# Relational graph layer on one core: A11 B11 by quarters in matrices one to three, index keys fetched earlier, and a new order for the fifth pair of row blocks

## The chip, the cores and the metric

The kernel runs on one core of one Trainium2 chip. The metric is the device time of one execution in microseconds (us), lower is better. TensorE is called PE below, VectorE DVE, ScalarE ACT, GpSimd POOL and SyncE SP, as in the profile.

## The reference

There are N = 1250 nodes with D = 1024 features, 20000 edges (src, dst) sorted by dst, and R = 8 edge types. Cut to what matters:

```python
h = maximum(layernorm(x), 0)
u = h @ root + bias
for r in range(8):                       # per type: mean over incoming edges, then a matrix
    mean_r = segment_sum(h[src] * (type == r), dst) / maximum(count_r, 1)
    u = u + mean_r @ weight[r]
z = concatenate([u, h]) @ w_gate + b_gate
out = x + tanh(u) * z + h * (1 - z)
```

All data are float32.

## The kernel before

**Matrices and steps.** The mean over edges is exchanged with the product: the kernel multiplies h with every weight matrix first, writes the results to DRAM (`y`), and then gathers the rows that the edges name. There are eleven 1024x1024 matrices, `mats`, numbered s: the eight weights (0 to 7), `root` (8), the lower half of `w_gate` (9) and its upper half (10, multiplied with u in a last stage of its own). h has ten blocks of 128 rows. They are taken as NP = 5 pairs, i = 0 to 4; pair i holds blocks i and i + 5. `step(s, i)` multiplies pair i with matrix s, and the order is s outside, i inside. The text writes step (s, i).

**One step.** `product` multiplies 256x1024 by 1024x1024 by the scheme of Strassen and Winograd: seven products of half size instead of eight. They are A11 B11, S1 T1, S2 T2, S4 B22, S3 T3, A12 B21 and A22 T4. The S are sums of quarters of h, made once (`h_op`); the T are differences of quarters of the matrix, made by DVE for each matrix (`make_t1` to `make_t4`). `p1` to `p7` in the code are these products in Winograd's numbering: p1 = A11 B11, p5 = S1 T1, p6 = S2 T2, p3 = S4 B22, p7 = S3 T3, p2 = A12 B21, and A22 T4 comes last. Each is `add`, line L404: four matmuls with 512 moving columns, which the profile shows as eight instructions (f32 goes through in two). The results go to the four quarters c11, c12, c21, c22 of two `row` tiles `t[0]`, `t[1]`: copies out of PSUM by ACT (c11 L452, c22 L463, c12 L483, the piece d of c22 L428, c21 L513), additions by DVE (L421, L429, L443).

**Second level.** For matrices s > 0, pairs 0 and 1 are joined, and pairs 2 and 3 (`paired`), so that one of the seven products of both can be split once more into seven products of quarter size (256 moving columns, line L217) instead of eight. `Second` does so for A12 B21 in matrices 1 to 9. `Third` does it for S4 B22 and `First` for A11 B11, before the change only in matrices s > EARLY = 3. Pair 4 has no partner. `First` is worked in two halves: `early()` (four quarter products) at the end of the step before, `late()` (three) in place of A11 B11 of the even step; the odd step finds its A11 B11 ready in PSUM. Its sums of matrix and of h (`sums`, `next_sums`, four DVE operations each) go to the tiles `room`.

**PSUM.** There are four banks `ps`, two `ps_b` (the running sum b that begins with A11 B11), one `ps_n`, one `ps_q`. In matrices 0 to 3, `ps_q` belongs to the index work below.

**Calls.** All engines' instructions are in program order (the schedule is by hand). After each product `done()` calls `between(j)`, j = 0 to 6 in each step. There the other work is put in: loads of the next matrix (`load_first`, `load_next`, `load_b22`, `load_b21`), its differences, the sums, and one piece of a generator.

**Index work.** In matrices 0 to 3 that generator is `index()`: it turns the edge list into a table of slots. `slots` handles the 157 columns of edges in 40 groups of four, one group in two calls. The first call of two has `one_hots` (ACT, L1023 and L1025) and `load_keys` (SP: `k_bc` and `l_bc`, 256 KB each); the second has on PE `look` (L1091) and `count` (L1037), and on DVE `pick` (L1099), `add_counts`, `residue` (L1076) and `place` (L1107, L1112); `to_los` (ACT, L1083 and L1084) turns `l_bc` into the one-hots `to_lo` that `look` of the same group multiplies in the next round. Then `order` ranks the nodes by their number of edges (`places`, twenty DVE operations L1175) and `rows_and_weights` has POOL scatter the ids and gather the table rows. From matrix 5 on the generator is `edges`: POOL gathers rows of `y` (L1315), and DVE adds them with weights (L1320).

**Places of a matrix.** `load_first` gives each matrix nine buffers in rotation; in the version before, B21 takes the buffer of the old B22, and T4 that of the old T3.

Of the kernel before, what the change touches and what calls it, by code (L numbers as in the profile page):

```python
# [19 lines left out]
def tile_rgcn_highway(  # L20
# [109 lines left out]
    class Factors:  # L130
# [55 lines left out]
    class Second:  # L186
# [22 lines left out]
        def left(self):  # L209
            nc.vector.tensor_add(self.s1, self.a21, self.a22)  # L210
# [177 lines left out]
    def product(aop, w, to, between=lambda j: None, last=None, pieces=1, whole=True,  # L388
                fill=None, second=None, third=None, inner=None, first=None, early=None, own=(),
                aside=None):  # L390
# [49 lines left out]
        def p2():  # L440
            a = held("ps_q")
            add(a, A12, True)
            nc.vector.tensor_add(c11, c11, a)  # L443
            done()

        def p1():
            if first is None:
                b = lead()
                add(b, A11, True)
            else:  # L450
                b = first.late() if inner.holds else first.to1
            nc.scalar.copy(c11, b)  # L452
            done()
            filled("first")
            return b

        def p5(c=None):
            if c is None:
                c = inner.hold() if inner and inner.holds else held("ps_n")
                add(c, S1, True)  # L460
            else:
                add(c, S1, ks=range(KQ // 2, KQ))
            nc.scalar.copy(c22, c)  # L463
            done()
            filled("fifth")
            return c

        if first and inner.holds and early is None and "first" not in fill:
            c = inner.hold()
            add(c, S1, True, ks=range(KQ // 2))  # L470
            b = p1()
            p5(c)
        elif first and inner.holds:
# [12 lines left out]
        if whole and not third:  # L486
            p3()
            d = p7()
            if not second:
                p2()  # L490
        else:
            def then():
                inner.then(c)
                done()
                filled("third")

            if early:
                then()
            d = p7()
            if third:  # L500
                last(d, 0)
            if not inner:
                p3()
            elif not early and not inner.holds:
                then()
        if early:
            early()
        if pieces == 1:
# [11 lines left out]
        done()  # L520
        filled("fourth")
# [27 lines left out]
    def step(s, i, between=lambda j: None, second=None):  # L549
# [23 lines left out]
        def beside(j):  # L573
            at_call[:] = i, j
            new = fac[s + 1]
            if i == 0 and s > 0 and j == int(thirds(s)):
# [11 lines left out]
            if coming and i > 1 and j == 2:  # L588
                first_sums()
            if two and (i, j) == (1, 6):  # L590
                Second(fac[s], 2).left()
            if (s, i, j) == (0, 0, 3) or (s > 0 and (i, j) == (3, int(thirds(s)))):
# [18 lines left out]
        def sums(j):  # L611
# [20 lines left out]
        if two:  # L632
# [46 lines left out]
            else:  # L679
# [4 lines left out]
                inner=q, first=waiting_first.get((s, i - i % 2)) if two else None,  # L684
                early=early if coming else None, own=("ps_q",) if s > EARLY and not two else ())
# [73 lines left out]
    def rows_and_weights(g):  # L759
# [16 lines left out]
        for d in range(ND):  # L776
            rows_of(idx[:, g, d, :], table_rows, node_key[:, g, d:d + 1])
            if d % 2:
                yield

    with ExitStack() as early:
# [155 lines left out]
        pid = ix1.tile([P, 1], F32, name="pid")  # L937
        less_pid = ix1.tile([P, 1], F32, name="less_pid")
# [6 lines left out]
        def columns():  # L945
# [54 lines left out]
            nc.vector.tensor_single_scalar(less_pid, pid, -1.0, op=OP.mult)  # L1000
            yield

        def slots(ix):
# [14 lines left out]
            def one_hots(j):  # L1018
# [13 lines left out]
                now[j] = dict(is_lo=is_lo, is_at=is_at)  # L1032
# [18 lines left out]
            def load_keys(j):  # L1051
                c0, m = j * CG, len(chunks(j))
                for name, of in (("k_bc", keys_dram), ("l_bc", los_dram)):
                    t = now[j][name] = ix.tile([P, CG, P], I32, name=name, bufs=3)
# [93 lines left out]
        def order():  # L1148

            with tc.tile_pool(name="sort", bufs=1) as sp:  # L1150

                nc.gpsimd.iota(ids, pattern=[[P, ND]], base=0, channel_multiplier=1)
                ids_f = sp.tile([P, ND], F32, name="ids_f")
                nc.vector.tensor_copy(ids_f, ids)
# [12 lines left out]
                for _ in range(4):  # L1167
# [3 lines left out]
                def places(g):  # L1171
                    for d in range(ND):
# [5 lines left out]
                        if d % 2:  # L1178
                            yield
                    nc.vector.tensor_copy(pos_i[:, g, :], pos[:, g * ND:(g + 1) * ND])  # L1180

                for g in range(G):
                    yield from places(g)
                    if g == 0:
                        for _ in rows_and_weights(0):
                            pass
# [92 lines left out]
    with ExitStack() as edges_part:  # L1279
# [4 lines left out]
        inner_pool = edges_part.enter_context(tc.tile_pool(name="inner", bufs=1))  # L1284
        room = [inner_pool.tile([P, 2, n], F32, name=f"inner{k}")
                for k, n in enumerate((H, H, P, P))]
        p5_room = inner_pool.tile([P, H], F32, name="inner4")
# [150 lines left out]
        def beside_group():  # L1438

            for _ in range(4):  # L1440
                yield
            passes_over()
            yield
            yield from rows_and_weights(1)
            yield
            yield
# [341 lines left out]
```

## Time and profile before

| | |
|---|---|
| time, median of 3 runs | 1342.91 us (1342.43 to 1347.58) |
| profiled execution: time, span | 1342.95 us, 1341.2 us (1.75 us lie outside the span) |
| granted PE clock in it | 0.998 |
| PE busy | 1328.3 us (99%), 4096 instructions |
| DVE busy | 931.1 us (69%) |
| ACT busy | 372.0 us (28%) |
| POOL busy | 573.8 us (43%) |
| DMA | 270.92 MB, 202 GB/s |

The profile is that of one execution. Its times are in microseconds from the start of the span. Ends of matmuls are modelled, since they overlap; so where PE's time is counted, the text takes the distance from one group's start to the next group's start. Step (1, 0) starts at about 139, matrix 4 at about 510, and the last stage at about 1208.

### The profile page before, as it was taken

What the parts mean: (1) busy time and instruction counts of PE and PEld (TensorE: products, weight loads), DVE (VectorE), ACT (ScalarE), POOL (GpSimd) and SP (SyncE); (2) the same over time, 40 slices, a digit from 0 to 9 for tenths busy, and PEclk for the clock granted to TensorE, in tenths of its full rate; (3) what the DMA queues carried; (4) which work ended last, traced back from release to release, by engine and by line L of the source; (5) the groups of instructions that cost most, each with busy time, mean ns of one, the idle gap of its engine ahead of it and who ended that gap; (6) DMA issues with size and microseconds to landing.
All of it is one profiled execution on the core that took longest, in us unless ns stands there. A gap on an engine that the chain in (4) does not pass through costs nothing.

```text
span 1341.2 us, 13172 instructions
## 1 busy us (share of the span) xinstructions
PE 1328.3 (99%) x4096; PEld 709.1 (53%) x4096; DVE 931.1 (69%) x1763; ACT 372.0 (28%) x786; POOL 573.8 (43%) x509
## 2 busy tenths in 40 slices
PE   9999999999999999999999999999999999999997
PEld 5444455455445545655655565565556556554443
DVE  7753744654572855347887978887778799867875
ACT  3334556465641111211121211122121111221210
POOL 0000454555556256201454645436355565725631
PEclk9999999999999999999999999999999999999999
DMA  8744487956872361133739778868778967879961
GB/s 313 275 182 158 85 138 154 215 87 110 168 177 30 101 172 46 51 127 126 246 118 334 236 251 324 313 222 279 274 265 297 344 202 241 287 272 286 345 170 59
DMA packets 104317, 270.92 MB, mean 202 GB/s; under 512 B 20100, under 2 KB 22354, under 8 KB 104112
## 3 DMA queue, kind: packets, MB, share of 16 engines
q1 hardware_dynamic: 44048, 119.85, 30.9%
q0 software_dynamic: 44064, 118.20, 28.1%
q10 hardware_dynamic: 16128, 31.98, 7.4%
q8 instruction: 32, 0.52, 0.2%
q14 instruction: 45, 0.37, 0.1%
HBM read 212.63 MB, written 75.49 MB: 215 GB/s over the span
## 4 chain that ended last, share of the span: by engine, by line
PE 89%; DMA 4%; issue 3%; DVE 2%; POOL 1%; ACT 0%; POOLq 0%; SPq 0%; DVEq 0%; ACTq 0%
PE ps_b L404 45%; PE ps L404 18%; PE ps L217 12%; PE ps_n L404 5%; PE ps_b L217 2%; PE ps_q L217 2%; PE ps_q L404 2%; PE ps_n L217 1%; DMA got<-y,idx 1%; DMA l_bc<-los_dram 1%; PE ps L369 1%; DMA hr_dram<-row 1%; DMA h_op<-in_L_gnn_b_gate_dram 0%; POOL out_dram L720 0%; DVE u L1320 0%
## 5 line engine op out<-in xcount | busy, mean ns | idle before, releaser
L404 PE MATMUL ps_b<-w,h_op 128*128 128x512 f32 x1560 | 701.9, 595 | 1.1 <-ACT row L483 0.8
L404 PEld LDWEIGHTS ps_b<-w,h_op 128*128 128x128 f32 x1560 | 291.6, 190 | 329.3 <-issue 318.0
L1315 POOL DMA_INDIRECT got<-y,idx x193 | 249.9, 1295 | 309.3 <-DVE u L1320 187.6
L1320 DVE SCALAR_TENSOR_TENSOR u<-got,w_of,u 128x1024 f32<-128x1024 f32 (+1 forms) x193 | 246.7, 1281 | 35.8 <-DMA got<-y,idx 33.3
L404 PE MATMUL ps<-w,h_op 128*128 128x512 f32 (+1 forms) x592 | 263.4, 588 | 1.0 <-ACT row L463 1.0
L1130 POOL DMA_INDIRECT table<-row_col,at_i x157 | 165.3, 1053 | 180.8 <-DVE at_i L1126 119.5
L404 PEld LDWEIGHTS ps<-w,h_op 128*128 128x128 f32 x592 | 111.3, 190 | 125.0 <-issue 120.8
L429 DVE TENSOR_TENSOR row<-row 128x512 f32<-128x512 f32 x53 | 36.6, 691 | 81.3 <-ACT row L428 81.2
L428 ACT COPY row<-ps_b 128x512 f32<-128x512 f32 x53 | 31.0, 585 | 199.5 <-PE ps_b L404 199.5
L513 ACT COPY row<-ps_b 128x512 f32<-128x512 f32 x49 | 28.6, 584 | 200.9 <-PE ps_b L404 179.7
L404 PE MATMUL ps_n<-w,h_op 128*128 128x512 f32 x176 | 80.1, 592 | 0.0
L217 PE MATMUL ps<-w,w 128*128 128x256 f32 x288 | 71.5, 381 | 0.2 <-DVE w L210 0.2
L483 ACT COPY row<-ps_b 128x512 f32<-128x512 f32 x54 | 31.6, 585 | 136.8 <-PE ps_b L404 136.6
L217 PE MATMUL ps<-w,h_op 128*128 128x256 f32 x264 | 68.3, 381 | 0.0
L217 PEld LDWEIGHTS ps<-w,w 128*128 128x128 f32 x288 | 54.2, 190 | 21.7 <-issue 14.3
L217 PEld LDWEIGHTS ps<-w,h_op 128*128 128x128 f32 x264 | 49.6, 190 | 24.3 <-issue 18.7
L1112 DVE SCALAR_TENSOR_TENSOR junk<-k_bc,key_col,before 128x128 f32<-128x128 int32 x157 | 54.9, 350 | 4.2
L452 ACT COPY row<-ps_b 128x512 f32<-128x512 f32 x54 | 31.7, 587 | 92.8 <-PE ps_b L404 87.1
L1099 DVE TENSOR_TENSOR own<-ps_q,is_at 128x160 f32<-128x160 f32 (+1 forms) x40 | 12.7, 317 | 62.4 <-PE ps_q L1037 58.1
L404 PEld LDWEIGHTS ps_n<-w,h_op 128*128 128x128 f32 x176 | 33.4, 190 | 39.5 <-issue 38.7
L463 ACT COPY row<-ps 128x512 f32<-128x512 f32 x37 | 21.6, 585 | 106.9 <-PE ps L404 96.8
L1023 ACT ACTIVATE is_lo<-io,less_lo 128x128 bf16<-128x128 f32 x157 | 50.1, 392 | 3.0 <-PE ps L404 2.3
(237 smaller groups left out, 1441.3 us busy)
## 6 DMA issues: line engine op xcount, KB each, us to landing
y<-row SPq DMA_DIRECT2D x72, 512.0 KB
w<-in_L_gnn_weight_dram ACTq DMA_DIRECT2D x21, 1024.0 KB
w<-in_L_gnn_weight_dram SPq DMA_DIRECT2D x10, 1024.0 KB
k_bc<-keys_dram SPq DMA_DIRECT2D x39, 256.0 KB
l_bc<-los_dram SPq DMA_DIRECT2D x39, 256.0 KB
w<-in_L_gnn_w_gate_dram ACTq DMA_DIRECT2D x6, 1024.0 KB
h_dram<-h_op SPq DMA_DIRECT2D x9, 512.0 KB
u<-in_L_gnn_bias_dram SPq DMA_DIRECT2D x9, 512.0 KB
```

What stands on the lines that cost most here:

```text
L217: nc.tensor.matmul(p, a[:, k, :], b[:, k, :], start=(fresh and k == 0), stop=(k == 1), skip_group_check=True)
L404: nc.tensor.matmul(b[:, at], aop[:, i, k, :], w.of[i][:, k, at], start=(fresh and k == 0), stop=(k == KQ - 1), skip_group_check=True)
L428: nc.scalar.copy(d, b)
L429: nc.vector.tensor_add(c22, c22, d)
L452: nc.scalar.copy(c11, b)
L483: nc.scalar.copy(c12, b)
L513: nc.scalar.copy(c21, b)
L1023: nc.scalar.activation(is_lo[:, i, :], io, AF.Abs, bias=less_lo[:, c0 + i:c0 + i + 1])
L1112: nc.vector.scalar_tensor_tensor(junk, o["k_bc"][:, i, :], key_col[:, c:c + 1], before, op0=OP.is_equal, op1=OP.mult, accum_out=rank[:, c: ...
L1130: ins = nc.gpsimd.indirect_dma_start(out=table[:, :], out_offset=bass.IndirectOffsetOnAxis(ap=at_i[:n, c:c + 1], axis=0), in_=row_col[:n, ...
L1315: nc.gpsimd.indirect_dma_start(out=t[:n], out_offset=None, in_=y[g][:, :], in_offset=bass.IndirectOffsetOnAxis(ap=at[:n, d, k:k + 1], axis=0),
L1320: nc.vector.scalar_tensor_tensor(u[:n], t[:n], w, u[:n], op0=OP.mult, op1=OP.add)
```

## The change

The change does the following.

1. `First` is used for all matrices s > 0 (`firsts`), so also for the pairs (0, 1) and (2, 3) of matrices 1, 2 and 3. `room` and `p5_room` move to a pool that lives all through. A new argument `head` (even step) takes the place of `inner.holds`.
2. The fifth pair, i = 4, has an order of its own in matrices 0 to 9 (`lone`): p1, p5, p6, the first half of A12 B21, S3 T3, the second half of A12 B21, `early` of the next matrix, A22 T4, and S4 B22 at the end. c22 is no longer copied out by ACT: DVE adds d to the bank c itself. B21 and T4 of a matrix change buffers.
3. The index work has its keys loaded two rounds earlier (`k_bc` in five buffers) and `to_los` one round earlier (`to_lo` in four). The ids are made in `columns`. `order` waits seven calls and not four, and ranks one column in a call and not two. `rows_and_weights(1)` follows at once and no longer stands in `beside_group`. Calls (1, 5) and (4, 4) get no index work; before, (4, 5) got none.
4. `Second.left` is cut in two. Its first two sums are made at call 3 (before: call 4 in matrices 1 to 3, call 5 after them), the other two at call 4 or 5. For s > 3, `right(2)` and `right(3)` move from call 4 to call 5. `make_t4` is at call 1 in all matrices s > 0 (before: call 0 in matrices 1 to 3).

The diff, cut to its core:

```diff
-                                  t2=p["t2"], b21=p["b22"], t4=p["t3"])
+                                  t2=p["t2"], b21=p["t3"], t4=p["b22"])
...
+        def next_left(self):
             nc.vector.tensor_sub(self.s3, self.a11, self.a21)
             nc.vector.tensor_sub(self.s4, self.a12, self.s2)
...
-            nc.vector.tensor_add(c22, c22, d)
+            nc.vector.tensor_add(c22, c if lone else c22, d)
...
-            nc.scalar.copy(c22, c)
+            if not lone:
+                nc.scalar.copy(c22, c)
...
-        if first and inner.holds and early is None and "first" not in fill:
-            c = inner.hold()
+        if first and head and early is None and "first" not in fill:
+            c = inner.hold() if inner else bank()
             add(c, S1, True, ks=range(KQ // 2))
             b = p1()
             p5(c)
...
-        if whole and not third:
+        if lone:
+            a = held("ps_q")
+            add(a, A12, True, ks=range(KQ // 2))
+            p7()
+            p2(a)
+        elif whole and not third:
...
         if early:
             early()
-        if pieces == 1:
+        if lone:
+            add(b, A22)
+            nc.scalar.copy(c21, b)
+            done()
+            p3()
+        elif pieces == 1:
...
+    def firsts(s):
+        return s > 0
...
-        if thirds(s) and i == 1:
+        if firsts(s) and i == 1:
             return s, 2
-        if thirds(s + 1) and i == NP - 1 and s + 1 < NM - 1:
+        if firsts(s + 1) and i == NP - 1 and s + 1 < NM - 1:
...
-            if i == 0 and s > 0 and j == int(thirds(s)):
+            if i == 0 and s > 0 and j == 1:
                 fac[s].make_t4()
...
-            if q and i % 2 == 0 and j == 3:
+            if two and i % 2 == 0 and j == 3:
                 waiting_first[s, i].fifth_to()
-                q.sums()
+                if i == 0:
+                    waiting[0][0].left()
+                if q:
+                    q.sums()
...
-            if coming and i > 1 and j == 2:
+            if coming and (i > 1 or not q) and j == 2:
                 first_sums()
...
-            for k in {2: (0, 1), 4: (2, 3)}.get(j, ()) if s > EARLY else (j,) if j < 4 else ():
+            for k in {2: (0, 1), 5: (2, 3)}.get(j, ()) if s > EARLY else (j,) if j < 4 else ():
                 e.right(k)
             if j == (5 if s > EARLY else 4):
-                e.left()
+                e.next_left()
...
-                for name, of in (("k_bc", keys_dram), ("l_bc", los_dram)):
+                for name, of, bufs in (("k_bc", keys_dram, 5), ("l_bc", los_dram, 3)):
...
-                to_lo = o["to_lo"] = ix.tile([P, CG, P], BF16, name="to_lo")
+                to_lo = o["to_lo"] = ix.tile([P, CG, P], BF16, name="to_lo", bufs=4)
...
+            load_keys(0)
             for j in range(ng + 3):
-                for f, of in ((one_hots, j), (load_keys, j - 1), (as_bf16, j - 2),
+                for f, of in ((one_hots, j), (load_keys, j + 1), (as_bf16, j - 2),
                               (None, None), (look, j - 3), (count, j - 1), (pick, j - 3),
                               (add_counts, j - 1), (residue, j - 2), (place, j - 3),
-                              (to_los, j - 2), (None, None)):
+                              (to_los, j - 1), (None, None)):
...
-                if s > 0 and (i, j) in ((0, 0), (NP - 1, 5)):
+                if s > 0 and (i, j) in ((0, 0), (1, 5), (NP - 1, 4)):
```

More of the change, by code (lines that the diff above doesn't have):

```diff
@@ L389, in product @@
                 fill=None, second=None, third=None, inner=None, first=None, early=None, own=(),
-                aside=None):
+                aside=None, head=False, lone=False):
         c11, c12 = to[0][:, :Q], to[0][:, Q:]
@@ L438, in held, with p2 @@
             return psum.tile([P, CG, P], F32, name=name, bufs=1).rearrange("p c k -> p (c k)")
-        def p2():
-            a = held("ps_q")
-            add(a, A12, True)
+        def p2(a=None):
+            if a is None:
+                a = held("ps_q")
+                add(a, A12, True)
+            else:
+                add(a, A12, ks=range(KQ // 2, KQ))
             nc.vector.tensor_add(c11, c11, a)
@@ L450, in p1 @@
             else:
-                b = first.late() if inner.holds else first.to1
+                b = first.late() if head else first.to1
             nc.scalar.copy(c11, b)
@@ L472, in product @@
             p5(c)
-        elif first and inner.holds:
+        elif first and head:
             c = p5()
@@ L485, in product @@
         filled("sixth")
-        if whole and not third:
+        if lone:
+            a = held("ps_q")
+            add(a, A12, True, ks=range(KQ // 2))
+            p7()
+            p2(a)
+        elif whole and not third:
             p3()
@@ L495, in then @@
                 filled("third")
-            if early:
+            if early and inner:
                 then()
@@ L503, in product @@
                 p3()
-            elif not early and not inner.holds:
+            elif not early and not head:
                 then()
@@ L519, in product @@
                 last(b[:, at], at.start, d[:, at])
-        done()
-        filled("fourth")
+        if not lone:
+            done()
+            filled("fourth")
     mats = [weight[r] for r in range(R)] + [root, w_gate[D:, :], w_gate[:D, :]]
@@ L591, in beside @@
                 Second(fac[s], 2).left()
+                Second(fac[s], 2).next_left()
             if (s, i, j) == (0, 0, 3) or (s > 0 and (i, j) == (3, int(thirds(s)))):
@@ L684, in step @@
                 inner=q, first=waiting_first.get((s, i - i % 2)) if two else None,
+                head=i % 2 == 0, lone=i == NP - 1,
                 early=early if coming else None, own=("ps_q",) if s > EARLY and not two else ())
@@ L779, in rows_and_weights @@
                 yield
+    room = [keep.tile([P, 2, n], F32, name=f"inner{k}") for k, n in enumerate((H, H, P, P))]
+    p5_room = keep.tile([P, H], F32, name="inner4")
     with ExitStack() as early:
@@ L937, in tile_rgcn_highway @@
         pid = ix1.tile([P, 1], F32, name="pid")
+        ids_f = ix1.tile([P, ND], F32, name="ids_f")
         less_pid = ix1.tile([P, 1], F32, name="less_pid")
@@ L1000, in columns @@
             nc.vector.tensor_single_scalar(less_pid, pid, -1.0, op=OP.mult)
+            nc.gpsimd.iota(ids, pattern=[[P, ND]], base=0, channel_multiplier=1)
+            nc.vector.tensor_copy(ids_f, ids)
             yield
@@ L1031, in one_hots @@
                                         op=OP.is_equal)
-                now[j] = dict(is_lo=is_lo, is_at=is_at)
+                now[j].update(is_lo=is_lo, is_at=is_at)
             def count(j):
@@ L1052, in load_keys @@
                 c0, m = j * CG, len(chunks(j))
-                for name, of in (("k_bc", keys_dram), ("l_bc", los_dram)):
-                    t = now[j][name] = ix.tile([P, CG, P], I32, name=name, bufs=3)
+                for name, of, bufs in (("k_bc", keys_dram, 5), ("l_bc", los_dram, 3)):
+                    t = now.setdefault(j, {})[name] = ix.tile([P, CG, P], I32, name=name,
+                                                              bufs=bufs)
                     nc.sync.dma_start(t[:, :m, :].rearrange("p c e -> p (c e)"),
@@ L1150, in order @@
             with tc.tile_pool(name="sort", bufs=1) as sp:
-                nc.gpsimd.iota(ids, pattern=[[P, ND]], base=0, channel_multiplier=1)
-                ids_f = sp.tile([P, ND], F32, name="ids_f")
-                nc.vector.tensor_copy(ids_f, ids)
                 val = sp.tile([P, NHI], F32, name="val")
@@ L1166, in order @@
                 nc.vector.memset(one, 1.0)
-                for _ in range(4):
+                for _ in range(7):
                     yield
@@ L1177, in places @@
                             op0=OP.is_gt, op1=OP.mult, accum_out=pos[:, c:c + 1])
-                        if d % 2:
-                            yield
+                        yield
                     nc.vector.tensor_copy(pos_i[:, g, :], pos[:, g * ND:(g + 1) * ND])
@@ L1183, in order @@
                     yield from places(g)
-                    if g == 0:
-                        for _ in rows_and_weights(0):
-                            pass
+                    for _ in rows_and_weights(g):
+                        pass
                 nc.vector.reduce_max(most[:, 0:1], runs, axis=AX.X)
@@ L1283, in tile_rgcn_highway @@
         drc = small.tile([P, ND], F32, name="drc")
[L1284 to L1287, printed above, removed]
         fresh = [GOT]
@@ L1438, in beside_group @@
         def beside_group():
-            for _ in range(4):
+            yield
+            passes_over()
+            for _ in range(5):
                 yield
[L1442 to L1446, printed above, removed]
             for g in range(G):
```

## The prediction

> **What bounds the kernel now.** I read the page's busy shares, then the groups, the waits of PE alone, the timeline by groups, and the chain where PE stood.
>
> ```profile
> PE 1328.3 (99%) x4096; PEld 709.1 (53%) x4096; DVE 931.1 (69%) x1763; ACT 372.0 (28%) x786; POOL 573.8 (43%) x509
> PE ps L404 <- ACT row L463: 1.0, 1, 1.0
> PE ps_q L1091 <- ACT to_lo L1084: 0.6, 1, 0.6
> PE ps L217 <- DVE w L210: 0.2, 1, 0.2
> ```
>
> The first line is the page: PE is busy for 99% of the span, no other engine for more than 69%. The other three are the waits of PE (line, releaser, us in total, times, longest): in all the matrices PE waits hardly at all, and three of its seven waits are at places that the change touches. So the time is the sum of PE's groups, plus these waits, plus what the change adds of new ones. The price of a group is its distance to the next one in the timeline (step (4, 4) and the start of (5, 0)):
>
> ```profile
> 615.68 3.60 PE L404 MATMUL ps_q<-w,h_op 128*128 128x512 f32 x8
> ...
> 619.11 1.03 PE L217 MATMUL ps<-w,h_op 128*128 128x256 f32 x4
> 619.97 1.03 PE L217 MATMUL ps<-inner,inner 128*128 128x256 f32 x4
> 620.84 1.03 PE L217 MATMUL ps_b<-w,h_op 128*128 128x256 f32 x4
> 621.70 1.03 PE L217 MATMUL ps<-inner,inner 128*128 128x256 f32 x4
> 622.56 3.60 PE L404 MATMUL ps_b<-w,h_op 128*128 128x512 f32 x8
> ...
> 627.71 1.03 PE L217 MATMUL ps<-inner,inner 128*128 128x256 f32 x4
> 628.58 1.03 PE L217 MATMUL ps_b<-w,inner 128*128 128x256 f32 x4
> 629.46 1.13 PE L217 MATMUL ps_b<-inner,h_op 128*128 128x256 f32 x4
> 630.42 1.88 PE L404 MATMUL ps_n<-w,h_op 128*128 128x512 f32 x4
> ```
>
> A product of eight instructions with 512 columns takes 619.11 - 615.68 = 3.43 us. The four groups from 619.11 are `early`, 3.45 us; the three from 627.71 are `late`, 2.71 us, of which 0.11 us is the wait of the third group for ACT's copy L353. That is `First` as matrices 4 to 9 run it already.
>
> **First in matrices 1 to 3.** Per joined pair two products A11 B11 go (2 x 3.43 = 6.87 us) and 3.45 + 2.71 = 6.16 us come: -0.71 us. Six pairs (two in each of three matrices): -4.2 us. A rule that speaks against it stands in the Trainium skill, "TensorE: Matmul & The Clock Gate", section "Back-to-back issue gap": spacing is set by the weight load as well as by the columns, about 81 ns at 128 and 131 ns at 512 columns. An estimate by a straight line between them puts 256 columns at 0.75 of the price of 512; then the seven small products would cost 28 x 0.75 x 0.429 = 9.0 us, every pair would lose 2.1 us, and the six 13 us. The row above has 0.216 us for 256 columns against 0.429 us for 512, a half; I go by the row.
>
> Beside PE the new work is per pair: DVE eight sums (2.2 us each four, rows L271 to L274), L348 and L360 of 0.43 us, together some 5.3 us; ACT two copies of 0.36 us and one of 0.57 us. Does it stay beside PE? In matrix 1 DVE was busy 17.3 of 22.8 us in step (1, 0), 10.1 of 23.0 us in the next and 13.1 of 30.0 us in the third stretch (busy time by stretches 139.2:162, 162:185, 185:215). The even step loses 0.72 us of PE and gains 0.4 us of DVE: 17.8 of 22. The odd step gets the sums of the next pair, 5.3 us: about 15 of 23. The deadlines: `next_sums` (2.2 us, after an addition of 0.43 us) must be done between the end of `early` and `late`. Between them lie A22 T4 and half of S1 T1, 3.43 + 1.72 = 5.15 us, after step 4 also S4 B22, 8.6 us. In calls (1, 5) and (4, 4) no index work is queued ahead of it. `make_t2` (2.28 us) is ahead of it in step 4; it hides under `early`. If that cover went, a late sum would cost up to 2.6 us each, 16 us for six.
>
> ACT is tighter. In step (s, 3) A11 B11 no longer stands first, and its copy c11 has to be out before S2 T2 may add to the bank. The timeline around 192 shows what is queued ahead of it:
>
> ```profile
> 192.21 0.58 ACT L452 COPY row<-ps_b 128x512 f32<-128x512 f32 x1 [1.87 <-PE ps_b L404]
> 192.69 1.28 ACT L1023 ACTIVATE is_lo<-io,less_lo 128x128 bf16<-128x128 f32 x4
> 194.00 0.63 ACT L1025 ACTIVATE is_lo<-is_lo 128x512 bf16<-128x512 bf16 x1
> 194.54 0.24 ACT L1069 CAST s_b<-seen 128x80 bf16<-128x80 f32 x1
> ```
>
> A copy starts 0.20 us after its product, one round of one-hots then ends 2.6 us later, `to_los` takes 0.72 + 0.63 us, c11 0.59 us: 4.8 us. PE meanwhile has a quarter product (0.86), `look` and `count` (0.22) and S1 T1 (3.5): 4.6 us. So some 0.2 us is waited for, in matrices 1 and 2. The same sum for e.sixth in step (s, 1) gives 5.2 against 5.5 us, no wait. I take 0.1 us for each of the six pairs, +0.6 us; bounds 0 (ACT always in time) and one round of ACT late, 2.6 us, for each of six: +16 us. The nearest rows, `look` and `count` met without wait all through matrices 1 and 2, put it at the low end.
>
> PSUM: the fifth step now holds c to its end, and a, x, y need the other three `ps` banks. If the next step had to take c's bank it would wait for L421, about 1 us, three times (+3 us); it takes one that has long been read (a's, after L443), so 0.
>
> **Index work earlier.** The chain in its order of time, around 343 and around 1064:
>
> ```profile
> 343.00 13.83 DMA l_bc<-los_dram
> 356.85 0.73 ACT to_lo L1083
> 357.60 0.63 ACT to_lo L1084
> ...
> 1064.36 8.25 DMA hr_dram<-row
> 1072.70 0.59 ACT row L463
> 1073.34 3.70 PE ps L404 x8
> ```
>
> `l_bc` came 13.8 us after its issue, ACT stood, and PE with it: the group before lasted 4.15 us in place of 3.43, `count` 0.36 in place of 0.12. That is 0.98 us. With the load two rounds and `to_los` one round ahead, load to use is about five calls, 18 us, and not three, 11 us: -0.98 us. Every round still has two loads on SP (39 to 40 of each), their buffers come free at the same distance, so y stores and `load_next` behind them meet the same waits: 0. That `look` needs `to_lo` is then covered by a whole round. DVE's waits for the ids (16.8 us) and for `v_bc` (6.1 us) go as well; PE did not stand for them: 0. `rows_and_weights(1)` puts some 20 indirect DMAs and two waits (about 26 + 10 us) on POOL in one piece, in (4, 0); behind it POOL has nothing until the first gather at 631.76, ahead of which it was idle for 80.8 us. The twenty L1175 (1.6 us each) come one in a call; four fall into step (4, 0); step (6, 0) carries nine L1320 of 1.28 us (741 to 764) with no PE wait: 0.
>
> **The fifth pair.** c22's copy L463 had to wait for a `row` tile whose store was issued at 1064.36 and took 8.25 us; PE waited 1.13 us and 0.10 us behind. In the new order the first write to that tile is the copy after S3 T3, 3.43 + 1.72 us later (from 1069.0 to after 1077), when the store has landed: -1.23 us. Between S2 T2 and S3 T3 lies 1.72 us where 3.43 lay; ACT's copy needs 0.85 us of it. The store of t[0] goes out at the end of the step, with that of t[1], about 4 us later than before; the first gather of `y` is added by DVE only at 639.6, about 4 us after it lands. 0 for both, +1 us at most. B21 is loaded at the same call as before; T4, made at call 1, is needed 13 us later.
>
> **Left sums earlier.** In step (9, 1) PE waited for L210 and L211 (1.20 and 0.97 us for groups of 0.86): -0.44 us. `right(2)`, `right(3)` move one call, with 7 us of cover.
>
> **The sum.** -4.24 - 0.98 - 1.23 - 0.44 + 0.6 = -6.3 us. The profiled execution took 1342.95 us (span 1341.2 us), as good as the median 1342.91: 1336.6 us. A measurement of this kernel tells about 0.5% from no change; that is 6.7 us, or 1336.2 us. The sum falls just short of it.
>
> **The rivals.**
> - *No new wait at all:* the sum without the 0.6, and without some small ones: 1335 to 1336.2, at 1336.0. For it speaks that `First` runs in matrices 4 to 9 with 0.11 us per pair; against it the ACT sum above. It is faster by just over the bound. 0.33.
> - *The waits come back elsewhere* (the store or the keys are waited for at another line, or ACT is late in most odd steps): only the products' 4.2 us remain or less, 1338.3 to 1349.6, at 1339.3. For it: DMA time to landing of `y` stores goes up to 16.5 us. 0.14.
> - *Slower:* DVE falls one round behind in the odd steps of matrices 1 to 3, which start without 3.43 us of A11 B11 of their own, and `look` (L1091) waits for `residue` (L1076). One round on DVE is 2.3 to 3.0 us (146.41 to 149.4 in the timeline). Six odd steps at 2.7 us: +16 us, 1352.8. It decides from 2.2 us per odd step (6.3 + 6.7 = 13 us). Against it: DVE has 4 us free in the even and 8 us in the odd step. 0.11.
>
> **How the numbers follow.** The forecast's case (1336.2 to 1338.3) has 0.42. Faster by over 0.5% is the first rival, 0.33; within 0.5% the forecast and the second, 0.56; slower the third, 0.11. The range 1335.2 to 1344.0 leaves out the slow rival and the far parts of the first two.
>
> **What would show it.** PE should have 2400 - 96 instructions of 512 columns and 1176 + 168 of 256. In matrices 1 to 3 groups ps_b<-inner,h_op of 0.97 us should appear twice per matrix. The wait for L463 and for L1084 should be gone from PE's waits, and the group before `look` near 348 be 3.43 us. A wait of PE for L452 in steps (1, 3) and (2, 3) would show the ACT sum right. It is wrong if PE waits for DVE L1076, L271 to L274 or L348, if `late` takes over 3 us, or if PE's total distance in matrices 1 to 3 falls by less than 4 us.

## The result

| | before | after |
|---|---|---|
| median | 1341.96 us (7 runs, 1340.64 to 1347.58) | 1337.4 us (7 runs, 1337.23 to 1337.77) |
| profiled execution: time, span | 1342.95, 1341.2 us | 1337.41, 1335.6 us |
| PE instructions of 512, of 256 columns | 2400, 1192 | 2304, 1360 |

After to before is 0.9961, 95% interval 0.9947 to 0.9975. The profiled executions differ by 5.54 us, the medians by 4.6; the sum said 6.3, from a profiled execution that took 1.0 us more than the median before in this table. The 256-column count has 16 instructions (of line L404, not of L217) that the prediction's 1176 did not hold, in both kernels; the difference is 168 as forecast. The seven times after lie within 0.6 us, those before within 7.

The page's PE line and all the waits of PE in the kernel after (line, releaser, us in total, times, longest). L406 is the old L404, L219 the old L217:

```profile
PE 1323.3 (99%) x4168; PEld 722.1 (54%) x4168; DVE 956.9 (72%) x1823; ACT 372.7 (28%) x794; POOL 568.5 (43%) x509
PE ps L722 <- POOL eps L724: 1.4, 1, 1.4
PE ps L371 <- DVE h_op L862: 0.8, 1, 0.8
PE ps_b L406 <- ACT row L489: 0.8, 1, 0.8
PE ps L371 <- DVE h_op L376: 0.7, 1, 0.7
PE ps_b L219 <- ACT ps_b L345: 0.6, 1, 0.6
PE ps_b L406 <- ACT h_op L378: 0.2, 1, 0.2
```

The three waits of before that the change touches are gone: for c22's copy, for `to_lo`, and for the left sums. Between 140 and 520 us this view lists no wait of PE. Two waits are new, the fourth and fifth. The chain through each of them, in order of time (start, us, what):

```profile
130.54 0.73 ACT to_lo L1116
...
131.93 1.18 ACT is_lo L1055 x4
...
134.00 0.28 ACT ps_b L345
...
134.32 1.13 PE ps_b L219 x4
...
1188.56 0.59 ACT h_op L430
...
1189.18 0.69 DVE h_op L431
1189.87 0.61 DVE h_op L376
...
1190.53 0.66 PE ps L371 x4
```

The first is step (0, 4): the first `early`, for matrix 1. Its copy L345 stands on ACT behind `to_los` and a round of one-hots, since call (4, 4) is kept free in matrices s > 0 only. PE's distance there is 0.715 us too long. The second is step (9, 4). Its new order holds c in a `ps` bank to the end; of the four transposes that follow (L371) the last needs a bank that is free only when DVE's copy L376 is done, and that stands behind L431, which waits for d (ACT L430). 0.853 us too long.

`late` in matrix 1, in PE's timeline:

```profile
145.90 1.03 PE L219 MATMUL ps_b<-w,inner 128*128 128x256 f32 x4
146.76 1.09 PE L219 MATMUL ps_b<-inner,h_op 128*128 128x256 f32 x4
147.69 1.88 PE L406 MATMUL ps<-w,h_op 128*128 128x512 f32 x4
```

The second group takes 147.69 - 146.76 = 0.93 us where its neighbour takes 0.86: the small wait for ACT that `First` has in matrices 4 to 9 too, below what the view of waits lists.

### The profile page after: what moved, and what is told of

The parts are those of the page before. It is cut to its first block, busy times and chain, and to the rows that moved or that the text cites. A ratio compares the mean times of both kernels' runs of the same rounds, so it can differ in the third digit from the quotient of the medians.

```text
span 1335.6 us, 13410 instructions
## 1 busy us (share of the span) xinstructions
PE 1323.3 (99%) x4168; PEld 722.1 (54%) x4168; DVE 956.9 (72%) x1823; ACT 372.7 (28%) x794; POOL 568.5 (43%) x509
## 4 chain that ended last, share of the span: by engine, by line
PE 85%; issue 4%; DVE 2%; DMA 2%; POOL 1%; ACT 0%; POOLq 0%; DVEq 0%; ACTq 0%
PE ps_b L406 41%; PE ps L406 17%; PE ps L219 14%; PE ps_b L219 4%; PE ps_n L406 4%; PE ps_q L219 2%; PE ps_n L219 2%; PE ps_q L406 2%; DMA w<-in_L_gnn_b_gate_dram 1%; DMA h_op<-z_dram,node 1%; POOL out_dram L746 1%; DVE row L1733 0%; DVE row L1734 0%; PE ps_q L1069 0%; PE ps_q L1124 0%
## 5 line engine op out<-in xcount | busy, mean ns | idle before, releaser
L406 PE MATMUL ps_b<-w,h_op 128*128 128x512 f32 x1464 | 659.6, 595 | 1.0 <-ACT row L489 0.8
L406 PEld LDWEIGHTS ps_b<-w,h_op 128*128 128x128 f32 x1464 | 273.6, 190 | 308.4 <-issue 297.4
L1339 POOL DMA_INDIRECT got<-y,idx x193 | 245.8, 1274 | 290.3 <-DVE u L1344 184.1
L406 PE MATMUL ps<-w,h_op 128*128 128x512 f32 (+1 forms) x592 | 264.8, 589 | 0.1
L406 PEld LDWEIGHTS ps<-w,h_op 128*128 128x128 f32 x592 | 111.0, 190 | 119.2 <-issue 115.0
L431 DVE TENSOR_TENSOR row<-row 128x512 f32<-128x512 f32 x44 | 30.3, 690 | 79.0 <-ACT row L430 79.0
L430 ACT COPY row<-ps_b 128x512 f32<-128x512 f32 x53 | 31.1, 586 | 194.1 <-PE ps_b L406 194.1
L406 PE MATMUL ps_n<-w,h_op 128*128 128x512 f32 x176 | 80.1, 592 | 0.0
L489 ACT COPY row<-ps_b 128x512 f32<-128x512 f32 x54 | 31.7, 586 | 163.6 <-PE ps_b L406 163.4
L219 PE MATMUL ps<-w,h_op 128*128 128x256 f32 x288 | 74.5, 381 | 0.0
L219 PE MATMUL ps<-w,w 128*128 128x256 f32 x288 | 71.1, 380 | 0.0
L529 ACT COPY row<-ps_b 128x512 f32<-128x512 f32 x40 | 23.4, 585 | 162.6 <-PE ps_b L406 142.3
L219 PEld LDWEIGHTS ps<-w,h_op 128*128 128x128 f32 x288 | 54.0, 190 | 27.1 <-issue 21.6
L219 PE MATMUL ps<-inner,inner 128*128 128x256 f32 x264 | 67.8, 379 | 0.0
L219 PEld LDWEIGHTS ps<-w,w 128*128 128x128 f32 x288 | 54.6, 190 | 21.8 <-issue 15.8
L219 PEld LDWEIGHTS ps<-inner,inner 128*128 128x128 f32 x264 | 50.2, 190 | 14.5 <-issue 8.4
L406 PEld LDWEIGHTS ps_n<-w,h_op 128*128 128x128 f32 x176 | 33.4, 190 | 39.5 <-issue 39.0
L457 ACT COPY row<-ps_b 128x512 f32<-128x512 f32 x54 | 31.7, 587 | 75.9 <-PE ps_b L406 71.3
```

Source lines behind the costliest of these rows:

```text
L219: nc.tensor.matmul(p, a[:, k, :], b[:, k, :], start=(fresh and k == 0), stop=(k == 1), skip_group_check=True)
L406: nc.tensor.matmul(b[:, at], aop[:, i, k, :], w.of[i][:, k, at], start=(fresh and k == 0), stop=(k == KQ - 1), skip_group_check=True)
L431: nc.vector.tensor_add(c22, c if lone else c22, d)
L489: nc.scalar.copy(c12, b)
L529: nc.scalar.copy(c21, b)
L1339: nc.gpsimd.indirect_dma_start(out=t[:n], out_offset=None, in_=y[g][:, :], in_offset=bass.IndirectOffsetOnAxis(ap=at[:n, d, k:k + 1], axis=0),
```

## The experiments

Each kernel is the kernel after with one edit, unless said otherwise. The kernel before ran on the same chip beside each group of four. `f1` ran with the `f` group; the `g` kernels are set against it too, though they ran later, when the kernel before took 1343.47 us (35 runs) and not 1344.33.

### The kernel after once more, and its parts undone

`f1_after_again` is unchanged.

> The kernel after, unchanged, beside the other kernels of this group, so that each of them can be set against it on the same chip. Theory (the products of matrices 1 to 3, about 5 us, plus the three old waits, less two new ones): 5.5 us below the kernel before, ratio 0.9959, with no wait of PE from 140 to 520 us. Rival: the gain belongs to the chip on which it was first seen; ratio 0.999 to 1.001.

Measured: 1338.7 us, before 1344.33 us (25 runs), ratio 0.9955 (0.9938 to 0.9972). The gain is there again, 5.6 us by the medians. Its profiled execution (span 1336.8 us) shows the two new waits at the same places and a third one of 0.93 us, at 960 us, which the first execution did not have; it is read below.

`f2_both` takes the two new waits away:

```diff
-                early=early if coming else None, own=("ps_q",) if s > EARLY and not two else ())
+                early=early if coming else None, own=(("ps_q", "ps_n") if s == NM - 2 else ("ps_q",)) if s > EARLY and not two else ())
...
-                if s > 0 and (i, j) in ((0, 0), (1, 5), (NP - 1, 4)):
+                if (s, i, j) == (0, NP - 1, 4) or s > 0 and (i, j) in ((0, 0), (1, 5), (NP - 1, 4)):
```

> The kernel after with both of its new waits taken away: call (0, 4, 4) gets no index work, so that ACT's copy L345 does not stand behind one-hots; and in step (9, 4) the bank c is ps_n, so that the fourth transpose of the last stage finds a free ps bank. Theory: 0.7 + 0.85 us go and nothing comes, 1.5 us below the kernel after (ratio to before 0.9948). Rival 1: the index work ends one call later and PE stands for it at another place, so that one wait is only moved: 0.7 to 0.9 us. Rival 2: without the wait the next one behind it is as late (DVE's additions ahead of the transposes): 0 us.

Measured: 1335.81 us (1335.45 to 1337.18), ratio 0.9934 (0.9915 to 0.9953), 2.9 us below `f1` by the medians, 1.9 us by the spans (1335.0). In its trace neither wait is left and nothing has come in their place from 120 to 150 us or at the transposes. The two edits were made together, but the traces keep them apart: where the transposes begin `f2` is 0.95 us ahead of `f1` (1188.64 for 1189.59), behind them 1.86 us (1190.38 for 1192.24). So both were waits on the path. All six of its runs lie below all eight of `f1`, so this version beats both kernels; the 1.5 us expected compare with 1.9 us in the traces and 2.9 us by the medians (the intervals of the two ratios overlap). What remains is the third wait of `f1`, here too:

```profile
PE ps L219 <- DVE inner L274: 0.8, 1, 0.8
```

It is in step (7, 4), at `early` for matrix 8. DVE stands before that for rows that POOL gathers (1.2 to 3.4 us for each of four, `got<-y,idx`), then makes a difference of the matrix (2.29 us), one addition, and only then the sums L273 to L276. In the first execution of the kernel after L274 ended at 958.50 and PE came for it at 959.38; here PE would have come at 958.59 and L274 ended at 959.47. The margin is under a microsecond, and gathered rows come sooner or later by as much.

`f3_first_from_four`:

```diff
     def firsts(s):
-        return s > 0
+        return s > EARLY
...
-                waiting_first[s, i].fifth_to()
+                if firsts(s):
+                    waiting_first[s, i].fifth_to()
```

> The kernel after, with First only from matrix 4 on, as in the kernel before; all else is as after. Theory (products are counted, 96 instructions of 512 columns come back for 168 of 256): six pairs lose 0.71 us each, 4.2 us, and the wait at 134 us (0.7 us) goes: 3.5 us above the kernel after. Rival 1: the sums of First cost time beside PE, which goes with them: 1 us above or less. Rival 2: with A11 B11 in one piece the index work gets cover back, and the time does not change at all.

Measured: 1341.49 us (1341.22 to 1342.69), ratio 0.9978 (0.9964 to 0.9991): 2.8 us above `f1`, and by the spans (1339.5 us) 2.7 above `f1`, 3.9 above the first execution of after. Without the chance wait of 0.93 at 960, which it does not have, that is 3.6 to 3.9 against 3.5 expected. The instruction counts are those of before. All ten of its runs lie above all eight of `f1`, though the intervals of the ratios overlap. So the products are a part of the gain, at about the price that the rows gave.

`f4_fifth_as_before`:

```diff
-                                  t2=p["t2"], b21=p["t3"], t4=p["b22"])
+                                  t2=p["t2"], b21=p["b22"], t4=p["t3"])
...
-                head=i % 2 == 0, lone=i == NP - 1,
+                head=i % 2 == 0, lone=False,
...
-                if s > 0 and (i, j) in ((0, 0), (1, 5), (NP - 1, 4)):
+                if s > 0 and (i, j) in ((0, 0), (1, 5), (NP - 1, 5)):
```

> The kernel after with the fifth pair's old order (S4 B22 before S3 T3, c22 copied out by ACT) and the old places of B21 and T4; the index work skips call (4, 5) again and not (4, 4). Theory: the wait of c22's copy for the store of its row tile at 1073 us (1.13 + 0.10 us) comes back, the wait of the fourth transpose (0.85 us) goes: 0.4 us above the kernel after, between -0.9 (store in time) and +1.3. Rival: the new order carries a part of the gain that the count does not show (waits in the fifth steps of all matrices): 2 us or more above.

Measured: 1339.68 us, ratio 0.9971 (0.9952 to 0.999), 1.0 us above `f1`, between 1337.82 and 1345.97: inside the theory's range, and not clear of noise. The expected trade is in its waits:

```profile
PE ps L406 <- ACT row L469: 1.2, 1, 1.2
```

That is c22's copy behind the store of its `row` tile, 1.32 us in PE's distance at 1068; the waits at 134, at 960 and for the fourth transpose are gone. This profiled execution (1337.82 us, the fastest of its ten) took 0.8 us less than that of `f1`. Over all runs the old order spreads over 8 us, the new one in `f1` over 3; that it is dearer in the median is not shown. The old order also explains the wait at 960: with it `early` comes after S4 B22, one product of 3.43 us later, and L274 (ended at 957.4) was 5.0 us ahead of PE (962.42). The new order spends that margin.

`g1_keys_as_before`:

```diff
-                for name, of, bufs in (("k_bc", keys_dram, 5), ("l_bc", los_dram, 3)):
+                for name, of, bufs in (("k_bc", keys_dram, 3), ("l_bc", los_dram, 3)):
...
-                to_lo = o["to_lo"] = ix.tile([P, CG, P], BF16, name="to_lo", bufs=4)
+                to_lo = o["to_lo"] = ix.tile([P, CG, P], BF16, name="to_lo")
...
-            load_keys(0)
...
-                for f, of in ((one_hots, j), (load_keys, j + 1), (as_bf16, j - 2),
+                for f, of in ((one_hots, j), (load_keys, j - 1), (as_bf16, j - 2),
...
-                              (to_los, j - 1), (None, None)):
+                              (to_los, j - 2), (None, None)):
```

> The kernel after, with the index keys loaded, and the one-hots of the low halves made, as late as in the kernel before (loads one round behind the one-hots in place of one ahead, three buffers of k_bc). Theory (a load of 13.8 us that comes late by turns is all that this part of the change removes): PE waits again for ACT L1117 once or twice, 0.7 to 2 us above the kernel after, more in single executions than in others. Rival 1: 5 us or more above, because with First in matrices 1 to 3 the odd steps have no A11 B11 of their own to wait behind, and every late load is waited for. Rival 2: no difference; the wait is an accident of one execution.

Measured: 1341.5 us (1338.87 to 1348.81), ratio 0.9977 (0.996 to 0.9994): 2.8 us above `f1`, more than the theory's 2 and less than the rival's 5 (the intervals of the two ratios overlap). The chain shows how:

```profile
164.98 11.55 DMA l_bc<-los_dram
...
177.94 0.48 ACT row L489
...
178.47 3.70 PE ps_b L406 x8
...
227.45 13.84 DMA l_bc<-los_dram
...
242.75 0.27 PE ps_q L1124 x4
```

Loads of 11.6 and 13.8 us hold ACT. The second is the wait of before (`look` waits for `to_lo`, 0.68 us). The first is one that before did not show: c12's copy L489 stands on ACT behind the `to_los` that waits, and PE loses 1.57 us. So a late load can cost through a copy that is queued behind the instruction that waits for it, not through `look` alone. The rest of this execution's difference (span 1340.1 us) is 0.18 us at 301 and a dearer wait at L274, 1.6 for 0.93 us.

`g2_left_as_before` makes the four sums in one call again (`e.left()` and `e.next_left()` together, the early call of `left()` at call 3 gone) and has `right(2)`, `right(3)` at call 4:

> The kernel after, with all four left sums of A12 B21 made in one call, as in the kernel before, and right(2), right(3) at call 4. Theory: only the wait in step (9, 1) comes back, 0.3 to 0.45 us above the kernel after, which its time can hardly show but PE's groups near 1105 can. Rival: in matrices 1 to 3, where the even steps now carry the sums of First too, DVE is late with them: 2 us or more above, with waits of PE for L210 to L213 in steps (1, 1) to (3, 3).

Measured: 1341.93 us, ratio 0.9989 (0.9974 to 1.0003), 3.2 us above `f1`. Both were wrong, the theory by the size and the rival by the place. Step (9, 1):

```profile
1106.86 0.42 DVE L210 TENSOR_TENSOR w<-h_op 128x256 f32<-128x256 f32 x1
...
1107.34 2.08 PE L219 MATMUL ps<-w,w 128*128 128x256 f32 x4 [2.53 <-DVE w L210]
1109.20 1.73 PE L219 MATMUL ps_q<-w,h_op 128*128 128x256 f32 x4
```

And the same place in the kernel before:

```profile
1109.69 0.41 DVE L210 TENSOR_TENSOR w<-h_op 128x256 f32<-128x256 f32 x1
...
1110.16 1.13 PE L217 MATMUL ps<-w,w 128*128 128x256 f32 x4 [0.17 <-DVE w L210]
```

PE is 2.69 us late there where it was 0.34 in the kernel before, though DVE's list from L184 to L210 is the same in both. DVE reaches L210 at 1106.86, 2.83 us sooner than in the kernel before (1109.69). PE reaches its group at 1104.64, 5.18 us sooner (1109.83). The difference of the two, 2.35 us, is what the wait has grown by. I read it so: PE comes sooner because matrices 1 to 3 are shorter (at the first `late` of matrix 4 it is 4.62 us ahead of the kernel before, 509.02 for 513.64) and because the wait at the store (1.23 us) is gone; DVE, which stood for gathered rows until 1077.65 and works without a gap from there, gained less. In the kernel before PE's later arrival had covered most of this. No run undoes two parts together, so this is argued from the two traces, not shown by an experiment. On top come seven distances of 0.427 to 0.59 us where 0.216 is normal, 1.6 us, and 0.6 us in step (8, 1).

So the parts don't seem to add up. Undone one at a time (`f3`, `f4`, `g1`, `g2`) they cost 2.8, 1.0, 2.8 and 3.2 us by the medians, 9.8 together, where the whole change brings 5.6. By the spans of the profiled executions it is 2.7, -0.8, 3.3 and 4.1, 9.3 together. Each ratio is uncertain by some 2 us, and `f1` stands in all four differences, so the single values are rough and the sum alone proves little. The traces say it more directly, in one execution each: PE loses 2.3 us at late keys in `g1` (1.57 and 0.68) where it lost about 1 in the kernel before, and 4.9 us at the left sums in `g2` (2.69, 0.6 and 1.6) where it lost 0.44. Both fit parts that protect what the others gained.

### How much room ACT and DVE have left

`g3_calls_filled`:

```diff
-                for _ in range(7):
+                for _ in range(13):
...
-                if s > 0 and (i, j) in ((0, 0), (1, 5), (NP - 1, 4)):
+                if s > 0 and (i, j) in ((0, 0),):
```

> The kernel after, with index work in calls (1, 5) and (4, 4) of matrices 1 to 3 too (six calls that the change keeps free); the ranking waits six calls longer, so that it starts no sooner. Theory (those calls are free because early's copies L345 and L347 on ACT would stand behind one-hots, as in matrix 0): a wait of 0.7 us at each early of matrices 1 to 3 whose call carries one-hots, two to five of them, 1.5 to 3.5 us above the kernel after. Rival 1: DVE is what they are free for: next_sums late by one group of index work, 2 us or more for each, 10 us above. Rival 2: no wait at all, and the free calls cost nothing and bring nothing: within 0.5 us.

Measured: 1341.12 us (1339.98 to 1344.36), ratio 0.9975 (0.9961 to 0.9989), 2.4 us above `f1`, the size that was expected, though the intervals of the two ratios overlap. But of three waits between 240 and 290 us only one is the theory's:

```profile
246.77 1.28 ACT L1055 ACTIVATE is_lo<-io,less_lo 128x128 bf16<-128x128 f32 x4 [4.42 <-DMA k_bc<-keys_dram]
...
258.26 0.36 ACT L345 COPY ps_b<-ps 128x256 f32<-128x256 f32 x1
...
265.30 2.29 DVE L176 TENSOR_TENSOR w<-w,w 128x2048 f32<-128x2048 f32 x1 [6.68 <-DMA w<-in_L_gnn_weight_dram]
```

L345 at 258.26 stands behind `to_los` and one-hots as in step (0, 4); PE is 0.63 us late. The other two begin with loads: `k_bc` took 18.25 us to come, ACT stood 4.42 us and L489 behind it cost PE 1.09 us; a matrix load came 18.9 us after its issue, DVE works without a gap from there to `residue`, and `look` cost PE 1.32 us at 279.8. The second hangs on the first: the matrix load is issued on ACT's queue at 246.35, just when ACT has its `k_bc`. Whether the filled calls cause the late key load or only lack the time to hide it was not tried.

`g4_ranks_twice` does the rank operations of `place` twice (`for _ in range(2)` around them):

> The kernel after, with the rank operations of place (L1145 and the one beside it, four in a group of 512 edges) done twice, some 1.6 us more on DVE in each of 40 groups, 64 us in all, on the engine that the slower rival of the prediction was about. Theory (DVE has 4 us free in an even step and 8 us in an odd step of matrices 1 to 3, and three groups fall into each step): 4.8 us more per step are just held, so PE waits in the even steps only, 0 to 1 us in each of six, up to 6 us above the kernel after. Rival: DVE has no room at the places that count (the sums of First and the residue ahead of look), and half or more of the 64 us shows: 30 us or more above.

Measured: 1345.41 us, ratio 1.0001 (0.9985 to 1.0017), 6.7 us above `f1`. DVE's busy time rose from 957.2 to 1011.8 us, so 54.6 us were added and about an eighth shows. That is just past the theory's end and far from the rival's.

```profile
290.18 0.29 PE L1124 MATMUL ps_q<-s_b,to_lo 128*128 128x40 bf16 x4 [2.00 <-DVE s_b L1109]
...
290.48 2.06 PE L219 MATMUL ps<-w,h_op 128*128 128x256 f32 x4
...
416.73 0.26 PE L1124 MATMUL ps_q<-s_b,to_lo 128*128 128x40 bf16 x4 [2.06 <-DVE s_b L1109]
416.83 1.11 PE L219 MATMUL ps<-w,h_op 128*128 128x256 f32 x4
```

The two largest waits are `look` behind `residue`, 2.2 us each, where the odd steps (2, 1) and (3, 1) begin; three smaller ones of 0.15 to 0.75 us lie in the 14 us before them. That is the mechanism of the prediction's slower rival, at its place and at the size per step from which it was to decide, but in two of six odd steps, and only with some 1.4 us (54.6 / 40) more on DVE in every group. The smaller three lie in even steps, where the theory had put them all.

### Four runs on a chip with interruptions

On another chip the kernel before takes 1375.18 us (35 runs, 1369.01 to 1384.84), and differences of a few microseconds are not to be read there. Four kernels ran on it: `e1_before_again` (the kernel before, unchanged), `e2_first_from_four`, `e3_both` and `e4_keys_as_before`, with the edits of `f3`, `f2` and `g1`. The kernel after itself did not run there.

> The kernel before, unchanged, for a second profiled execution. Theory (PE's time is the sum of its groups and of a few waits): the groups are the same; of the three waits that went, the one for the left sums (0.44 us, engines only) is there again, while the two that hang on a DMA's landing (0.98 us at the keys, 1.23 us at the row store) may be there or not, so that the profiled time is between 1340.3 and 1343 us. Rival (the waits are fixed by the order of instructions): all three are there again with the same sizes, 1342.9 us.

> The changed kernel, but A11 B11 by quarters only from matrix four on, as before; the rest of the change stays. Theory: the six pairs give back 6 x 0.71 = 4.2 us, and the wait for ACT's copy in the early part after matrix 0 (0.72 us) goes, so 3.5 us slower than the changed kernel, 1340.9 us. Rival (most of the gain came from the index work and the order of the fifth pair): less than 2 us slower, below 1339.4 us.

> The changed kernel with two small edits: call 4 of step (0, 4) gets no index work, and the fifth pair of matrix 9 takes its bank c from ps_n, so that the four transposes find four ps banks. Theory: the two waits of PE that the changed kernel has gained (0.72 us and 0.85 us) go, 1.5 us faster than the changed kernel, 1335.9 us. Rival (the index calls shift by one, so that ACT comes late somewhere else; the transposes wait for DVE's copies anyway): 0.0 to 0.5 us faster, 1337 us.

> The changed kernel, but the keys are loaded and made into one-hots as late as before (three buffers of k_bc, two of to_lo). Theory: ACT stands at to_lo in some rounds, and as the odd steps no longer begin with 3.43 us of their own, PE stands with it at least once, 0.7 to 3 us slower than the changed kernel, 1338 to 1340.5 us. Rival (PE's wait at the keys was an accident of one execution): no wait of PE at look, 1337.4 us.

Measured: 1372.63 us (ratio 0.9972, 0.9944 to 0.9999), 1370.15 (0.9955, 0.9929 to 0.9981), 1374.99 (0.9996, 0.9968 to 1.0023), 1384.13 (1.0051, 1.0019 to 1.0083). The same kernel against itself gives 0.9972, with an interval that leaves out 1, so the first three tell nothing apart: the expected 3.5 us of `e2` and 1.5 us of `e3` can't be seen, though in `e3`'s trace the two waits are gone. In the index phase of all four the chain is interrupted again and again: that of each has two to six lines of 3.7 to 11.5 us like this one of `e3` (the line names no cause):

```profile
331.33 7.98 another core or an unknown queue
```

There PE waited 6.8 us at `late`. The chains of before, after, and the `f` and `g` kernels show no such line in the index phase, and what it comes from stays open. One thing can be read with some caution: with the keys loaded late (`e4`) the kernel is slower than before there, by about 0.5%, and its interval touches only that of `e3`. That would fit late keys that cost most where everything comes late, but it is not shown.

## Why the prediction was right, point by point

The time, 1337.4 us, lies in the forecast's own case (1336.2 to 1338.3); the sum was 0.8 us too good. With what the trace shows in place of each term: -4.95 (products: 96 x 0.4292 saved, 168 x 0.2158 added) + 0.43 (in the six `late`, five times 0.064 and once 0.105) - 0.98 - 1.23 - 0.44 + 0.715 + 0.853 = -5.6 us; measured -5.5. That the time lies so near is in part luck: the 0.6 us for a wait that did not come made up for part of the 1.57 us of two that were not seen. `f2`, without these two, took 1335.81 us on its chip, which is the time of the first rival (1335 to 1336.2).

- **First.** Right in mechanism and size (-4.95 + 0.43 = -4.5 us for -4.24), shown by the counts, by `late` and, within its noise, by `f3`. It is the largest term in this count of PE's distances. Half the price for half the columns, as the row had it, held for the new groups too: 0.216 us for 256 columns beside 0.429 us for 512. The estimate of 0.75, a straight line through the two figures in the Trainium skill, "TensorE: Matmul & The Clock Gate", section "Back-to-back issue gap", does not hold here: the measurement decides against it.
- **ACT in the odd steps, +0.6 us.** This term was wrong: no wait came. In step (1, 3) the ends look like this:

```profile
216.74 1.03 PE L219 MATMUL ps<-w,h_op 128*128 128x256 f32 x4
...
216.94 0.59 ACT L529 COPY row<-ps_b 128x512 f32<-128x512 f32 x1 [3.06 <-PE ps_b L406]
217.43 1.28 ACT L1055 ACTIVATE is_lo<-io,less_lo 128x128 bf16<-128x128 f32 x4
...
220.16 0.63 ACT L1117 ACTIVATE to_lo<-to_lo 128x512 bf16<-128x512 bf16 x1
...
220.70 0.57 ACT L457 COPY row<-ps_b 128x512 f32<-128x512 f32 x1
...
221.56 3.68 PE L406 MATMUL ps_b<-w,h_op 128*128 128x512 f32 x8
```

  From the end of the product (216.74) to the end of c11's copy (220.70 + 0.57) ACT took 4.53 us, not 4.8: some ACT instructions in a row overlap by about 0.1 us (the copy from 216.94 ends at 217.53, the next starts at 217.43), and the sum had added most of them in full. PE took 4.82 us to S2 T2 (221.56), not 4.6: two pairs of `look` and `count` come between (217.61 and 221.34), and the sum had one. So ACT is 0.3 us early where the sum had it 0.2 us late.
- **The two waits that came.** "it takes one that has long been read (a's, after L443), so 0" holds for the five-product steps that follow in the matrices, not for step (9, 4), behind which four transposes take four banks: the step that failed is the PSUM term, which looked at one bank and one successor. "In calls (1, 5) and (4, 4) no index work is queued ahead of it" was said for DVE and all matrices; the diff's condition has s > 0, and the first `early` stands in matrix 0, on ACT's queue. `f2` shows both: 1.57 us counted as PE's distances, 1.86 us between its trace and that of `f1`.
- **Keys.** The wait is gone as forecast. Its two pieces, 0.72 and 0.24 us, make 0.96 us and not 0.98. That the part is worth this was the reading of one execution: undone in the changed kernel it costs 2.3 us in the trace (1.57 and 0.68) and 2.8 us by the medians, as ACT's copies wait too (`g1`). In matrices 1 to 3 ACT's idle time for `l_bc` was 9.0 us in the kernel before and is 1.0 us after.
- **Fifth pair.** The store's wait is gone, and `f4` brings it back at 1.32 us for 1.23. "0 for both" of its costs missed that `early` comes 3.43 us sooner and so nearer to its sums; the 0.9 us at 960 that some executions have is the price.
- **Left sums.** -0.44 us was right as an account of before and wrong as the worth of the part: 3.2 us in the changed kernel (`g2`), by the reading above because PE comes to that place sooner and DVE does not by as much.
- **The slower rival.** DVE held. In the two stretches from 139 us the even step grew from 17.3 to 18.5 us of 22.4, the next from 10.1 to 14.4 of 23.0, as the text had it (17.8 and 15). `g4` shows how far it was: with some 1.4 us more per group the rival's waits appear, and the whole gain is gone.

## What to carry to other kernels

When the saturated engine gets faster, it comes sooner to the places where it waits for others: a wait of 0.34 us was 2.69 us here with the other parts in. So the worth of removing one wait, read from the old profile, can be too low; undo parts from the changed kernel as well as adding them to the old one. When work is put at a new place, walk every queue at the first and the last turn of the loop, where a guard like s > 0 or another successor changes what stands ahead of it. A late transfer can delay every copy out of PSUM that stands on its reader's queue behind the reader, not only the reader.

## What the runs showed of the hardware

After a wait of PE of more than 2 us the granted clock can fall to half, and the next matmuls take twice their distance. In `g4` busy times and granted clock by stretches (PE, weight loads, DVE, ACT, POOL, then the clock, the DMA share and GB/s):

```profile
290.00:294.00 4.00, 3.83 (x17) 3.17 (x17) 3.75 (x22) 2.88 (x7) 3.09 (x4) 0.57 0.68 123
...
416.00:420.00 4.00, 3.27 (x16) 2.35 (x16) 3.72 (x23) 0.75 (x3) 3.09 (x4) 1.00 1.16 153
```

After the wait of 2.16 us at 290 seven distances were 0.43 to 0.57 us where 0.216 is normal, 1.6 us lost on top; the granted clock was 0.50 from 290.22 to 293.63 (0.57 is the mean of the 4 us). After the wait of 2.22 us at 416 it stayed at 1.00. In `g2` it was 0.50 from 1107.21 to 1110.62. So such a wait cost up to 1.75 times its length (2.16 and 1.6 us), and not every time.

The Trainium skill, "TensorE: Matmul & The Clock Gate", section "Part 1: The HAM clock gate (the "warmup" mystery)", has a clock that falls to half after an idle window of about 3.4 us and comes back after a busy one, with windows that run freely. The half rate and the 3.4 us agree with the traces, and so do free windows: in each of the 14 traces the changes of the granted clock lie whole multiples of 3.413 us apart, and half rate lasted 3.41 or 6.83 us each time before the last stage. That a whole idle window is needed does not agree. On that grid the wait that ended at 290.18 lies within one window, and the one that ended at 416.73 is cut by a window's end at 416.51, which leaves 2.00 us in the first. An estimate from the starts of the matmuls, over the windows at full clock of all 14 traces up to 1300 us, fits this: the 21 windows in which PE stood for 2.15 us or more were each followed by half rate, and the 38 in which it stood for 1.0 to 2.10 us by none. No run moves one wait against the window, so this is read from the traces and not shown by an experiment.
